# Graph network layer on one core: TensorE's first pass with a one-column second layer under a condition, and twelve empty instructions ahead of its loop

## Chip, cores and metric

One core of one Trainium2 chip. The time is the device time of one execution in microseconds. The kernel before took 271.45 us, the median of 3 runs (270.98 to 272.32).

## What is computed

There are 12,500 nodes with 128 features each, and 412,500 edges with 48 features each, sorted by the node they point at (`dst`). All nodes belong to one graph.

```python
h   = maximum(layernorm(x), 0)                       # 12500 x 128
agg = segment_sum(edge_attr, dst, 12500)             # 12500 x 48
u   = graph_globals[0]                               # 64
hid = relu(concat([h, agg, u]) @ W1 + b1)            # 12500 x 256
out = x + hid @ W2 + b2                              # 12500 x 128
```

Everything is f32.

## The kernel before

**Tiles.** The nodes are taken in 12 rounds of 1,024, and what is left is done in an epilogue. In each round the nodes are two blocks, A and B, of 512. The edges of a round are 11 groups of 3,072 rows in six slots (buffers e0 to e5, `SLOTS`), slot 4 with one group and the others with two.

**What a round does for the edges.** VectorE compares each edge's node with a row of numbers and so makes a one-hot matrix (`oh`, L666). TensorE multiplies edges and one-hots into windows of 28 nodes (`su`, L685, into PSUM banks `s`; even slots use one bank, odd slots the other). ScalarE copies the result to SBUF (`ss`, L689), and TensorE adds it at its place among the round's nodes (`pc`, L707, into banks `ax` and `ay`), with a second one-hot that VectorE makes (`pl`, L672). ScalarE copies the finished sums (`ag`, L750).

**What a round does for the nodes.** VectorE makes the statistics (`st`, L714, and small operations up to L731), ScalarE normalises (`xn`, L735), TensorE transposes (`tu`, L744), ScalarE copies (`hT`, L745). The first layer is `hh` (L754, from the nodes) and `ha` (L759, from the edge sums), in four PSUM banks `ph0`, `ph1`, `pt`, `po`, and a ReLU on ScalarE (`hi`, L764, into `hid`). The second layer `w2` (L780) multiplies `hid` by W2 into `ph0` for A and `ph1` for B, 8 matmuls of 128 columns each. VectorE adds the node's own row and b2, prepared by GpSimd as `xb` (L739), and keeps the result in `hold` (L784); all held rows are stored in the epilogue.

**The order.** A class `Flow` records every operation with what it reads and writes, and works out the semaphore waits. A round's body is written so that the second layer of round i stands in the body of round i + 1, behind the place matmuls of slots 5, 0 and 1. In round 0 there is no earlier round: the second layer there multiplies buffers that ScalarE has filled with zeros in the prologue, and VectorE writes the result into a held row that is written again later. TensorE's loop has its own shape: its body is cut at `su3`. It makes 13 passes, j = 0 to 12. The part from `su3` on stands first and is run if j > 0; then the prologue's part of TensorE, if j < 1; then the part up to the second layer, if j < 12. So in pass 0 TensorE runs the prologue, `su0` to `su2`, three placements and `w2A`, `w2B`, jumps back, and begins pass 1 with `su3`. In the order of the program, the jump stands right behind `w2B`, and the epilogue behind that.

**What waits for what around there.** `su5` writes the bank that the copy of `su3` reads. That copy stands in ScalarE's order behind the norms of A and B. The loads of the next x blocks are issued from ScalarE's queue, behind the copies `hT` and ahead of the copies `ag`; the load of a block waits until GpSimd's `xb` has read it, which starts when VectorE's `hold` has read the old `xb`. The edges come through SyncE's queue: each slot is loaded again when its `su` has read it.

In TensorE's order, matmuls stand as in the source; in the profile each f32 matmul is two weight loads and two matmul instructions (a transpose one of each).

Of the kernel before, what the change touches and what calls it, by code (L numbers as in the profile page):

```python
# [18 lines left out]
P = 128  # L19
# [9 lines left out]
R = 4  # L29
# [25 lines left out]
class Flow:  # L55
# [14 lines left out]
    def op(self, eng, name, reads, writes, emit, dma=False):  # L70
        self.seq.append(dict(eng=eng, name=name, r=tuple(reads), w=tuple(writes), emit=emit, dma=dma, it=self.at))
# [119 lines left out]
    def run(self):  # L191


        lo, hi = self.loop
        nc = self.nc
        start = [o for o in self.seq if o["it"] is None or o["it"] < lo]
        body = [o for o in self.seq if o["it"] == lo]
        end = [o for o in self.seq if o["it"] is not None and o["it"] > hi]
        for e in self.of:
            self.prepare(e)  # L200
        self.straight([o for o in start if o["eng"] != "PE"])
        regs = {}
        for o in body:
            for n, back in self.body.get(o["name"], []):
                u = self.unit(n)
                key = (o["eng"], u, (self.at_lo[n] - lo - back + self.extra[n]) * u)
                if key not in regs:
                    r = self.of[o["eng"]].alloc_register(f"w_{o['eng']}_{len(regs)}")
                    self.of[o["eng"]].reg_mov(r, key[2] + lo * u)
                    regs[key] = r  # L210

        def ahead(e):
            for n, c in sorted(self.ahead[e].items()):
                self.of[e].wait_ge(self.sem[n], (self.rank[n, c] + self.extra[n]) * self.unit(n))

        def repeat(o, i):
            waits = []
            for n, back in self.body.get(o["name"], []):
                u = self.unit(n)
                waits.append((self.sem[n], regs[(o["eng"], u, (self.at_lo[n] - lo - back + self.extra[n]) * u)]))  # L220
            self.emit(o, waits, i)

        def count(e):
            for (f, u, _), r in regs.items():
                if e == f:
                    self.of[e].reg_add(r, r, u)

        others = [e for e in self.of if e != "PE"]
        for e in others:
            ahead(e)  # L230
        every = {o["name"] for o in self.seq if o["it"] == hi}
        with nc.Fori(lo, hi + 1, 1, engines=[self.of[e].engine for e in others]) as i:
            for e in others:
                mine = [o for o in body if o["eng"] == e]
                for always, some in groupby(mine, lambda o: o["name"] in every):
                    with ExitStack() as last:
                        if not always:
                            last.enter_context(self.of[e].If(i < hi))
                        for o in some:
                            repeat(o, i)  # L240
            for e in others:
                count(e)
        own = [o for o in body if o["eng"] == "PE"]
        cut = [o["name"] for o in own].index(self.mark)
        with nc.Fori(0, hi - lo + 2, 1, engines=[nc.tensor.engine]) as j:
            with nc.tensor.If(j > 0):
                for o in own[cut:]:
                    repeat(o, None)
                count("PE")
            with nc.tensor.If(j < 1):  # L250
                self.straight([o for o in start if o["eng"] == "PE"])
                ahead("PE")
            with nc.tensor.If(j < hi - lo + 1):
                for o in own[:cut]:
                    repeat(o, None)
        self.straight(end)


# [149 lines left out]
def kernel(  # L408
# [12 lines left out]
    nc = tc.nc  # L421
# [4 lines left out]
    NH = H // P  # L426
# [19 lines left out]
    def bank(name):  # L446
        return psum.tile([P, BN], F32, name=name)
# [4 lines left out]
    ph = [bank("ph0"), bank("ph1")]  # L452
# [22 lines left out]
    hid = [const.tile([P, NH, r, P], F32, name=f"hid{k}") for k, r in two]  # L475
# [11 lines left out]
    w2 = const.tile([P, NH, D], F32)  # L487
# [25 lines left out]
    f = Flow(nc, tc)  # L513
    op = f.op
    A, B, Z = 0, 1, 2
# [62 lines left out]
    def dst_1(b):  # L578
        rows, n, g0 = dst_shape(b)
        d = di[b]  # L580
        k = f"di{b}"
        src = [k] + ([k + "r", k + "s"] if b == NB - 1 else [])
        op("DVE", f"fc{b}", src, [f"fc{b}"], lambda i: [nc.vector.tensor_copy(fc[b][:rows], d[:rows, 0:1])])
        k = b % DF
        op("DVE", f"df{b}", src + [f"fc{b}"], [f"df{k}"], lambda i: [
            nc.vector.tensor_scalar(df[k][:rows], d[:rows], fc[b][:rows], (V - 1) / 2, OP.subtract, OP.subtract)])
        op("DVE", f"mf{b}", [f"fc{b}", "m4"], [f"mf{b}"], lambda i: [nc.vector.tensor_scalar(mf[b][:rows], m4[:rows], fc[b][:rows], None, OP.mult)])

    def dst_2(b):
        rows, n, g0 = dst_shape(b)  # L590
        ob, ok = (ph[1], "PH1") if b else (S[0][:, P:], "S0")
        op("PE", f"of{b}", [f"mf{b}", "aq"], [ok], lambda i: [
            nc.tensor.matmul(ob[:, g0:g0 + n], aq[:rows].rearrange("c k n -> c (k n)"), mf[b][:rows, :n], start=True, stop=True, skip_group_check=True)])
        dv = df[b % DF].rearrange("c (p t) -> c t p", t=T)
        rv = rel[:, b * P * T:(b * P + rows) * T].rearrange("p (c t) -> p t c", t=T)
        for t0 in range(0, T, 3):
            key, bk = (("PT", pt), ("PH0", ph[0]), ("PO", po))[(2 * b + t0 // 3) % 3]
            pv = bk[:, :3 * P].rearrange("p (t c) -> p t c", t=3)
            op("PE", f"td{b}.{t0}", [f"df{b % DF}", "ident"], [key],
               lambda i, t0=t0, pv=pv: [nc.tensor.transpose(pv[:, t, :rows], dv[:rows, t0 + t, :], ident[:rows, :rows]) for t in range(3)])  # L600
            op("ACT", f"cd{b}.{t0}", [key], [f"rel{b}.{t0}"], lambda i, t0=t0, pv=pv: [nc.scalar.copy(rv[:, t0:t0 + 3], pv[:, :, :rows])])
# [190 lines left out]
    def prologue():  # L792
# [4 lines left out]
        for s in range(NS):  # L797
# [31 lines left out]
        blank = lambda name, key, dst_ap, shape: op("ACT", name, ["zero"], [key], lambda i: [  # L829
            nc.scalar.copy(dst_ap, zero[:shape[0]].to_broadcast(shape) if len(shape) == 2 else zero[:shape[0], :, None].to_broadcast(shape))])  # L830
        op("ACT", "c1", ["eps"], ["sc0"], lambda i: [nc.scalar.activation(sc[0][:, 0:1], eps, AF.Sqrt, bias=eps)])
        for k in (A, B):
            for a in range(NH):
                blank(f"hidz{k}.{a}", f"hid{k}.{a}", hid[k][:, a], [P, R, P])
            blank(f"xbz{k}", f"xb{k}", xb[k], [P, R, D])
        f.chain("DVE", "nm", [], ["nmod_i", "nmod"],
            lambda: nc.vector.tensor_scalar(nmod_i, nmod_i, NV - 1, None, OP.bitwise_and),
# [3 lines left out]
            lambda: nc.vector.tensor_reduce(a4, ident.rearrange("c (g k) -> c k g", k=CG), AX.X, OP.add),  # L841
            lambda: nc.vector.tensor_copy(aq, a4[:, :, None].to_broadcast([P, CG, NV])))
        op("DVE", "c3", ["iota_v"], ["iota_v"], lambda i: [nc.vector.tensor_scalar(iota_v, iota_v, 0.5, None, OP.mult)])
        for b in range(NB):
            dst_1(b)
            dst_2(b)
# [4 lines left out]
                             start=(t == 0), stop=(t == T - 1), skip_group_check=True)  # L851
# [120 lines left out]
    flags = nc.alloc_registers("bad")  # L972
    flag_of = {r.engine: r for r in flags}
    prologue()
    for it in range(NIT):
        body(it)
# [2 lines left out]
    ends = [f"ot{k}" for k in range(3)] + [f"x{k}" for k in (A, B)] + [f"hold{k}.{j}" for k in (A, B) for j in range(NIT - 1)]  # L979
    op("SP", "end", [], ends, lambda i: [nc.sync.nop(nofuse=True)])  # L980
    f.order((0, NIT - 1))
    f.mark = "su3"
    tc.mark_branch_hint_location("skip", engines=[ET.PE, ET.DVE])
    with tc.tile_critical(no_gpsimd_drain=True):
        f.run()
# [33 lines left out]
```

## Time and profile before

| what | value |
|---|---|
| median of 3 runs | 271.45 us (270.98 to 272.32) |
| profiled execution, its own time | 272.44 us |
| its span, first to last instruction | 270.7 us |
| busy: TensorE / VectorE / ScalarE / GpSimd | 92% / 88% / 47% / 20% |
| mean granted TensorE clock | 0.976 |
| DMA | 94.33 MB, mean 348 GB/s |

Rows of a timeline give the start in the span, the length, the engine, the line, the operation with output and input, and the number of instructions in a merged row; in brackets the idle time ahead of it and what ended that. Rows of the chain give start, length and what. Rows of stretches give, per engine in the order TensorE, its weight loads (PEld), VectorE, ScalarE, GpSimd, the busy time and the number of instructions, then the granted clock, the DMA share and GB/s. Rows of one line's instructions have shortest, median and longest duration in ns. Rows of the waits have the total in us, how often, and the longest. A row of a DMA queue has packets, MB and the share of time of 16 DMA engines.

### The profile page before, as it was taken

The numbers are of one execution on the slowest core, as the hardware profiler recorded it, in microseconds if no ns is written. First come the engines' busy times: TensorE is split into PE (matmuls) and PEld (weight loads), VectorE is DVE, ScalarE is ACT, GpSimd is POOL, SyncE is SP. The second block draws the span as 40 slices with busy tenths as digits, with TensorE's granted clock in tenths as the row PEclk, the third lists the DMA queues.
The fourth block names the chain that finished last, engine by engine and source line by source line (L and its number), as shares of the span: only waits on it lengthen the run. The fifth ranks groups of instructions, "written<-read, shape, count | busy, mean of one in ns | idle before, by whom it ended". The sixth has DMA issues, their size and how long they took to land.

```text
span 270.7 us, 17205 instructions
## 1 busy us (share of the span) xinstructions
PE 249.3 (92%) x7567; PEld 193.7 (72%) x7568; DVE 239.1 (88%) x591; ACT 127.6 (47%) x316; POOL 54.5 (20%) x47
## 2 busy tenths in 40 slices
PE   0853999999999999999999999999999999999990
PEld 0843894985977958949859769679589498597580
DVE  4699998998998999989989999989999899899511
ACT  6630524644545437337345445364383473454520
POOL 8100050050050230400500501403205005007000
PEclk9996699999999999999999999999999999999997
DMA  6999999999999999999999999999999999979911
GB/s 200 304 390 385 364 387 392 349 390 384 360 392 346 387 393 333 387 393 340 389 393 335 390 351 383 392 339 386 393 330 390 393 336 390 390 246 380 350 41 66
DMA packets 79012, 94.33 MB, mean 348 GB/s; under 512 B 3227, under 2 KB 72189, under 8 KB 78998
## 3 DMA queue, kind: packets, MB, share of 16 engines
q1 hardware_dynamic: 75398, 87.63, 92.4%
q10 hardware_dynamic: 3312, 6.03, 5.8%
q0 software_dynamic: 288, 0.49, 0.7%
q8 instruction: 7, 0.11, 0.2%
q14 instruction: 7, 0.06, 0.1%
HBM read 87.75 MB, written 6.40 MB: 348 GB/s over the span
## 4 chain that ended last, share of the span: by engine, by line
PE 88%; SPq 5%; DMA 3%; issue 1%; DVE 0%
PE s L685 27%; PE ph L780 18%; PE ph L754 8%; PE ax L707 8%; SPq L520 5%; PE ph L759 5%; PE pt L754 4%; PE po L754 4%; PE pt L759 4%; PE ay L707 3%; DMA e<-in_edge_attr_dram 3%; PE pt L744 3%; PE po L744 2%; PE s L942 1%; PE s L754 0%
## 5 line engine op out<-in xcount | busy, mean ns | idle before, releaser
L666 DVE TENSOR_TENSOR oh<-iota_v,rel_i 128x1344 f32<-128x1344 f32 (+1 forms) x78 | 130.5, 1712 | 0.3 <-PE s L685 0.3
L685 PEld LDWEIGHTS s<-e,oh 128*28 128x28 f32 x6336 | 73.2, 108 | 18.5 <-issue 16.4
L685 PE MATMUL s<-e,oh 128*28 128x48 f32 x6336 | 77.7, 208 | 7.5 <-issue 5.8
L739 POOL TENSOR_TENSOR xba<-xa,b_sb 128x512 f32<-128x512 f32 x12 | 15.5, 1290 | 193.6 <-DVE holda L784 193.6
L689 ACT COPY ss<-s 128x96 f32<-128x96 f32 (+1 forms) x72 | 17.0, 236 | 65.8 <-PE s L685 65.8
L672 DVE TENSOR_SCALAR pl<-iota_w,off_i 128x186 f32<-128x186 f32 x141 | 35.0, 308 | 0.5
L739 POOL TENSOR_TENSOR xbb<-xb,b_sb 128x512 f32<-128x512 f32 x12 | 31.1, 2594 | 0.0
L764 ACT ACTIVATE hida<-ph,bias 128x512 f32<-128x512 f32 x12 | 8.2, 687 | 41.4 <-PE ph L759 41.4
L780 PEld LDWEIGHTS ph<-w,hida 128*128 128x128 f32 x208 | 24.8, 195 | 3.9 <-issue 3.9
L707 PE MATMUL ax<-pl,ss 128*48 128x186 f32 (+3 forms) x172 | 27.3, 300 | 0.0
L780 PE MATMUL ph<-w,hida 128*128 128x128 f32 x208 | 27.3, 285 | 0.0
L707 PE MATMUL ay<-pl,ss 128*48 128x186 f32 (+3 forms) x168 | 26.4, 298 | 0.0
L780 PE MATMUL ph<-w,hidb 128*128 128x128 f32 x208 | 25.4, 275 | 0.0
L780 PEld LDWEIGHTS ph<-w,hidb 128*128 128x128 f32 x208 | 24.3, 192 | 0.0
L707 PEld LDWEIGHTS ax<-pl,ss 128*48 128x48 f32 x172 | 17.6, 126 | 4.3 <-issue 2.0
L735 ACT ACTIVATE xna<-xa,sha,sca 128x128 f32<-128x128 f32 x48 | 19.8, 484 | 1.0 <-DVE sha L731 1.0
L735 ACT ACTIVATE xnb<-xb,shb,scb 128x128 f32<-128x128 f32 x48 | 19.6, 481 | 0.0
L707 PEld LDWEIGHTS ay<-pl,ss 128*48 128x48 f32 x168 | 17.8, 124 | 0.0
L714 DVE BATCH_NORM_STATS2 sta<-xa 128x6 f32<-128x128 f32 x48 | 10.5, 280 | 6.1 <-DMA xa<-in_x_dram 6.1
L759 PE MATMUL ph<-ags,w1a 48*128 48x512 f32 x48 | 13.5, 641 | 0.0
L754 PE MATMUL ph<-hta,w1h 128*128 128x512 f32 x24 | 13.5, 645 | 0.0
L754 PE MATMUL po<-htb,w1h 128*128 128x512 f32 x24 | 12.3, 592 | 0.0
(150 smaller groups left out, 300.2 us busy)
## 6 DMA issues: line engine op xcount, KB each, us to landing
e<-in_edge_attr_dram SPq DMA_DIRECT2D x133, 576.0 KB, 7.7
xa<-in_x_dram ACTq DMA_DIRECT2D x11, 256.0 KB, 5.3
xb<-in_x_dram ACTq DMA_DIRECT2D x11, 256.0 KB, 5.8
out_dram<-holda SPq DMA_DIRECT2D x11, 256.0 KB, 3.5
out_dram<-holdb SPq DMA_DIRECT2D x11, 256.0 KB, 3.5
holda<-in_dst_dram SPq DMA_DIRECT2D x4, 384.0 KB, 5.0
e<-in_edge_attr_dram SPq DMA_DIRECT2D x1, 720.0 KB, 4.3
xa<-in_x_dram SPq DMA_DIRECT2D x1, 256.0 KB, 9.5
```

Of the source, the lines that this page charges most:

```text
L520: return [f.of[eng].dma_start(dst_ap(i) if callable(dst_ap) else dst_ap, src_ap(i) if callable(src_ap) else src_ap)]
L666: op("DVE", f"oh{name}", reads + ["iota_v"], [f"oh{name}"], lambda i: [nc.vector.tensor_tensor(ov, iota_v[:, None, None, :].to_broadcast([ ...
L672: nc.vector.tensor_scalar(out[:, j], iota_w, o[j], None, OP.is_equal) for j in range(len(o))])
L685: nc.tensor.matmul(S[k][NV * c:NV * c + V, j * DE:(j + 1) * DE], o[:, (j * CG + c) * T + t], ev[:, j * CG + c, t * DE:(t + 1) * DE], start ...
L689: op("ACT", f"ss{name}", [f"S{k}"], [f"ss{name}"], lambda i: [nc.scalar.copy(sv.rearrange("p j d -> p (j d)"), S[k][:, :m * DE])])
L707: out.append(nc.tensor.matmul(agg[bk][h:h + DE, at:at + w], sv[:, j], pv[:, j, frm:frm + w], start=bk in fresh and bk not in seen, stop=Tr ...
L735: nc.scalar.activation(xn[k][:m, r], xt[k][:m, r], AF.Relu, bias=sh[k][:m, r:r + 1], scale=sc[k][:m, r:r + 1]) for r in range(RR[k])])
L739: nc.gpsimd.tensor_tensor(xb[k][:m], xt[k][:m], b2_sb[:m, None, :].to_broadcast([m, RR[k], D]), OP.add)])
L744: op("PE", f"tu{k}", [f"xn{k}", "ident"], [key], lambda i: [nc.tensor.transpose(pv[:, r, :m], xn[k][:m, r], ident[:m, :m]) for r in range( ...
L754: nc.tensor.matmul(o, w1h[:, a * P:(a + 1) * P], hT[k][:, :, :m], start=first, stop=False, skip_group_check=True)])
L759: nc.tensor.matmul(o, w1a[h:h + DE, a * P:(a + 1) * P], ag[k // 2][h:h + DE, :, :m], start=False, stop=True, skip_group_check=True)])
L780: nc.tensor.matmul(ov[:m, r], hid[k][:, a, r, :m], w2[:, a], start=(a == 0), stop=(a == NH - 1)) for r in range(RR[k]) for a in range(NH)])
```

## The change

```diff
+        for _ in range(self.pad):
+            nc.tensor.nop(nofuse=True)
         own = [o for o in body if o["eng"] == "PE"]
...
             with nc.tensor.If(j < hi - lo + 1):
-                for o in own[:cut]:
-                    repeat(o, None)
+                for brief, some in groupby(own[:cut], lambda o: o["name"] in self.brief):
+                    some = list(some)
+                    if not brief:
+                        for o in some:
+                            repeat(o, None)
+                        continue
+                    with nc.tensor.If(j < 1):
+                        for o in some:
+                            repeat(dict(o, emit=self.brief[o["name"]]), None)
+                    with nc.tensor.If(j > 0):
+                        for o in some:
+                            repeat(o, None)
...
         for k in (A, B):
-            for a in range(NH):
-                blank(f"hidz{k}.{a}", f"hid{k}.{a}", hid[k][:, a], [P, R, P])
+            blank(f"hidz{k}", f"hid{k}.0", hid[k][:, 0, 0], [P, P])
...
+        op("DVE", "phz", [], ["PH0", "PH1"], lambda i: [nc.vector.memset(ph[k], 0.0) for k in (A, B)])
...
-    f.mark = "su3"
+    f.mark, f.pad = "su3", 12
+    f.brief = {f"w2{k}": lambda i, k=k: [nc.tensor.matmul(ph[k][:, 0:1], hid[k][:, 0, 0], w2[:, 0, 0:1], start=True, stop=True)] for k in (A, B)}
```

In pass 0 the second layer is one matmul of one column for each block, in place of 8 of 128 columns. In passes 1 to 11 it is as before, but behind a comparison of the pass number. VectorE clears the two banks in the prologue, and ScalarE clears only the part of `hid` that the short matmul reads. New lines move nearly all old ones behind them down by 12.

TensorE's order, from the last placements to the first instructions of the epilogue, before (`ax`, `ay`: sums in place; `ph_70`, `ph_71`: the banks ph0 and ph1; `w_143`: W2):

```order
L707 MATMUL ax<-pl_94,ss_100 48x186
L707 MATMUL ay<-pl_94,ss_100 48x186
L780 MATMUL ph_70<-w_143,hida 128x128 x8
L780 MATMUL ph_71<-w_143,hidb 128x128 x8
L253 UNCONDITIONAL_BRANCH
L245 REGISTER_ALU
L245 COMPARE_AND_BRANCH
L942 MATMUL s_65<-e_74,oh_87 28x48 x24
```

The same place in the changed kernel:

```order
L719 MATMUL ax<-pl_94,ss_100 48x186
L719 MATMUL ay<-pl_94,ss_100 48x186
L262 COMPARE_AND_BRANCH
L995 MATMUL ph_70<-w_143,hida 128x1
L995 MATMUL ph_71<-w_143,hidb 128x1
L262 UNCONDITIONAL_BRANCH
L265 COMPARE_AND_BRANCH
L792 MATMUL ph_70<-w_143,hida 128x128 x8
L792 MATMUL ph_71<-w_143,hidb 128x128 x8
L265 UNCONDITIONAL_BRANCH
L247 REGISTER_ALU
L247 COMPARE_AND_BRANCH
```

Two short matmuls, two comparisons and a jump are new ahead of the 16 matmuls of the second layer.

The start of TensorE's program up to the head of its loop, in the changed kernel:

```order
L1018 ISA
L1027 UNCONDITIONAL_BRANCH
L1027 BRANCH_PREFETCH_HINT
L1027 UNCONDITIONAL_BRANCH
L532 UNCONDITIONAL_BRANCH
L247 UNCONDITIONAL_BRANCH
L248 COMPARE_AND_BRANCH
L697 MATMUL s_66<-e_77,oh_90 28x48 x48
```

These are the rows of the kernel before with other line numbers: the twelve empty instructions of the source stand nowhere in TensorE's order.

VectorE's prologue in the changed kernel, from the last constants to the first use of `dst` (`holda` holds it there):

```order
L853 COPY aq<-a_157 128x128
L854 TENSOR_SCALAR iota_v<-iota_v 128x28
L855 MEMSET ph_70 128x512
L855 MEMSET ph_71 128x512
L595 CAST fc_159<-holda 128x1
L598 TENSOR_SCALAR holda<-holda,fc_159 128x768
```

The two memsets are new; the rows around them stand as before.

## Prediction

> **What bounds the kernel now.** I read the page's busy table and its chain that ended last, then the chain in order of time, then each engine's timeline around the first pass (15 to 46 us), where the change acts.
>
> ```profile
> PE 249.3 (92%) x7567; PEld 193.7 (72%) x7568; DVE 239.1 (88%) x591; ACT 127.6 (47%) x316; POOL 54.5 (20%) x47
> 24.19 0.85 PE s L685 x29
> 25.03 2.50 issue
> 27.53 1.64 PE s L685 x67
> 31.21 4.35 PE ph L780 x32
> 50.62 3.77 PE ph L780 x32
> 54.39 2.74 PE s L685 x240
> 64.52 0.42 PE pt L759
> 64.95 3.42 PE s L685 x284
> 69.46 3.77 PE ph L780 x32
> ```
>
> From 27.53 us on, the chain holds TensorE's work alone: each piece starts where the last one ended, and one pass takes 69.46 - 50.62 = 18.84 us. VectorE, with 88%, is close behind; what slack it has in a pass is worth as much as TensorE's own length. The row at 31.21 is the one the change removes: the second layer in pass 0, before any first layer has run, 32 matmul instructions for 16 matmuls (an f32 matmul is two).
>
> **The change part by part.** Pass 0 in TensorE's timeline, with three rows for the prices of what takes its place:
>
> ```profile
> 31.14 2.63 PE L780 MATMUL ph<-w,hida 128*128 128x128 f32 x16
> 35.49 2.81 PE L685 MATMUL s<-e,oh 128*28 128x48 f32 x240
> 38.22 0.65 PE L744 MATMUL pt<-ident,xna 128*128 128x128 f32 x4
> 44.13 1.13 PE L759 MATMUL ph<-ags,w1a 48*128 48x512 f32 x4
> 15.59 0.60 PE L860 MATMUL ph<-u,w1u 64*128 64x1 f32 x4
> 31.14 1.22 PE L780 MATMUL ph<-w,hida 128*128 128x128 f32 x4
> L780 PE MATMUL ph<-w,hida x208: 275/275/582, 31.1 to 261.4; 128*128 128x128 f32 x104
> 28.00:31.00 3.00, 3.00 (x67) 2.40 (x59) 2.84 (x10) 1.08 (x4) 0.00 (x0) 0.50 1.09 340
> 31.00:35.60 4.60, 4.60 (x44) 4.34 (x45) 4.53 (x10) 2.64 (x7) 0.00 (x0) 0.85 1.08 385
> ```
>
> *Removed and added.* The block runs from 31.14 to 35.49: 4.35 us. Two one-column matmuls, four instructions, replace it. The one-column row took 0.60 us for four; but the granted clock is 0.50 up to 31 and 0.85 on average over 31.00 to 35.60, so it is half until about 31 + 4.6 x 0.15 / 0.5 = 32.4. At that clock four instructions with the same weight load took 1.22 - 0.58 (the longest single one) = 0.64 from first start to fourth, 0.21 apart. So 0.60 to 0.85; I take 0.85, the row at the clock that holds there. The sums of slots 3 to 5 then start at 31.14 + 0.85 = 32.0: 3.5 us ahead.
>
> *Clock.* The first 0.4 us of these sums now run at half clock: 0.2 lost (0 if the clock returns early). The 240 instructions take 38.22 - 35.49 = 2.73: 1.09 for slot 3 (96 of them), 0.55 for slot 4, 1.09 for slot 5. Slot 5 could start at 32.0 + 0.2 + 1.64 = 33.8.
>
> *What is late next: ScalarE.* Slots 3 and 5 share a PSUM bank, so slot 5 waits for the copy of slot 3 (L689), which stands behind the norms on ScalarE.
>
> ```profile
> 32.01 1.63 ACT L735 ACTIVATE xnb<-xb,shb,scb 128x128 f32<-128x128 f32 x4
> 36.78 0.24 ACT L689 COPY ss<-s 128x96 f32<-128x96 f32 x1 [3.14 <-PE s L685]
> L520 SPq DMA_DIRECT2D e<-in_edge_attr_dram x1: 390/390/390, 24.7 to 24.7; - x1
> DMA to landing us min/median/max: 7.7/7.7/7.7
> ```
>
> The norms end at 33.64, set by VectorE and not by this change; the copy that now waits 3.14 us for TensorE would start there and end at 33.88. Slot 5 then starts near 33.95 instead of 33.8. Its last edges (issued 24.7, landed 7.7 later, 32.4) are there. The transposes start at 33.95 + 1.09 = 35.05: 38.22 - 35.05 = 3.15 us ahead.
>
> *Late after that: GpSimd.* The load of xb (in ScalarE's queue, ahead of the two copies L750 that L759 needs) waits until GpSimd has read the old xb.
>
> ```profile
> 35.24 0.68 DVE L784 TENSOR_TENSOR holda<-ph,xba 128x512 f32 x1
> 37.26 2.58 POOL L739 TENSOR_TENSOR xbb<-xb,b_sb 128x512 f32<-128x512 f32 x1
> 56.63 2.59 POOL L739 TENSOR_TENSOR xbb<-xb,b_sb 128x512 f32<-128x512 f32 x1
> 59.63 0.58 ACT L750 COPY ags<-ax 48x512 f32<-48x512 f32 x1 [0.80 <-POOL xbb L739]
> 60.23 0.58 ACT L750 COPY ags<-ay 48x512 f32<-48x512 f32 x1
> 62.97 1.13 PE L759 MATMUL ph<-ags,w1a 48*128 48x512 f32 x4
> ```
>
> GpSimd starts after VectorE's holda, which ran at 35.24 with no wait ahead of it, so it stays, and xbb ends at 39.84. In the next pass the copies began 59.63 - 59.22 = 0.41 after xbb and the second ended 1.59 after it; so in pass 0 it ends at 41.43. L759, now 44.13, could start at 44.13 - 3.15 = 40.98, but its second stream waits until about 41.45: 0.45 lost. What remains is 3.15 - 0.45 = **2.7 us**. In the second pass the same wait has 62.97 (the start of L759 there) - 60.81 = 2.2 of slack, less 2.7, plus what VectorE has gained by then (below): about even.
>
> *VectorE must follow.* It stands idle in each pass, 6.1 us in all, for xa, which is loaded behind TensorE's transposes:
>
> ```profile
> DVE sta L714 <- DMA xa<-in_x_dram: 6.1, 11, 1.0
> 46.49 0.87 DVE L714 BATCH_NORM_STATS2 stb<-xb 128x6 f32<-128x128 f32 x4
> 54.61 0.68 DVE L784 TENSOR_TENSOR holda<-ph,xba 128x512 f32 x1
> xb<-in_x_dram ACTq DMA_DIRECT2D x11, 256.0 KB, 5.8
> ```
>
> With xa issued earlier that 6.1 goes (1.0 in the first wait). What is left is a ring without TensorE: stb to the end of holda 55.29 - 46.49 = 8.8, then GpSimd 59.22 - 55.29 = 3.93, then xb's load 5.8: 18.5 us, just under 18.84. So VectorE follows, and the 2.7 lasts to the end, where ScalarE and VectorE wait for TensorE already.
>
> *The conditions.* Passes 1 to 11 now meet two compare-and-branches ahead of the real block. The trace has such rows at two places: where a pass begins (64.52 + 0.42 = 64.94, next piece 64.95: two compares and a jump) and at the loop's end (50.62 + 3.77 = 54.39, next 54.39). Nothing shows there: I read it as branches taken while matmuls already handed over still run. Ahead of the block those are the place matmuls, about 1.1 us of work; a wait of the weight loads stands there already:
>
> ```profile
> 50.55 1.86 PEld L780 LDWEIGHTS ph<-w,hida 128*128 128x128 f32 x16 [0.28 <-issue]
> ```
>
> So 0 to 0.28 a pass; I take 0, the rows with branches in them.
>
> *Prologue.* VectorE clears two banks, each at most the 0.68 of a 128x512 pass, in a gap:
>
> ```profile
> 2.77 0.17 DVE L843 TENSOR_SCALAR iota_v<-iota_v 128x28 f32<-128x28 f32 x1
> 4.17 0.15 DVE L583 CAST fc<-holda 128x1 f32<-128x1 int32 x1 [1.23 <-DMA holda<-in_dst_dram]
> ```
>
> At most 1.36 against the 1.23 of waiting, so 0 to 0.1 late, and later waits for dst follow; without that gap it would be 1.4 on VectorE. I take 0. ScalarE's clears only get shorter, ahead of the chain. The empty instructions leave no row in the built program (nothing stands for them in TensorE's order), so they cost nothing and shift nothing.
>
> Sum: 4.35 - 0.85 - 0.2 - 0.15 - 0.45 = 2.7. The profiled execution took 272.44 (span 270.7), 1.0 above the median of 271.45; taken off the median, **268.8 us**.
>
> **The rivals.**
>
> *The jump back is not covered.* TensorE's program arrives in blocks, seven packets in all:
>
> ```profile
> 21.15 1.76 PE L685 MATMUL s<-e,oh 128*28 128x48 f32 x97 [3.33 <-issue]
> q8 instruction: 7, 0.11, 0.2%
> q8 instruction: 1, 0.02, 68.1%
> q8 instruction: 1, 0.02, 68.8%
> ```
>
> The rows are the matmuls behind an earlier stop, all packets of the run, and those in the tenths of a microsecond from 25.1 and from 31.7. After the one at 25.1 TensorE, idle since 25.03, went on at 27.53, 2.4 later. The other lies in the middle of the block to be removed, whose 4.35 us would hide such a stop until 34.15. If the jump to the loop's head has to wait for it, the sums start at 34.15, 1.3 us ahead instead of 3.5, nothing else binds, and the time is 270.1. Against: TensorE ran 97 + 29 matmuls with their weight loads, 252 instructions, from one stop to the next; counted on by as much, the next block begins about 15 matmuls into the epilogue, and is what came at 31.7; the head of the loop has been there since the start, and no later pass fetches. The Trainium skill ("Runtime: NRT & Kernel Launch", section "Instruction fetch mechanics") says that a taken branch to a target outside a window of two pages stops until it is fetched; by that rule the stop is certain. The trace speaks against it: no packet came between 32 and 253 us, through eleven jumps back. Chance 0.14.
>
> *The branches show (slower).* If too little is handed over where the two compares stand, each of eleven passes pays for them. Up to 0.25 us a pass there is a gain left (11 x 0.25 = 2.7); from 0.37 (4.1 us) the kernel is over 0.5% slower; at 0.45, 4.95 - 2.7 gives 273.7. For it: no row shows a branch behind matmuls as short as the place ones. Against: the two boundaries with none. The Trainium skill ("Advanced Engine Details and Errata", section "Control Flow Timing") gives about 108 ns for a compare-and-branch; uncovered, an estimate of 11 x 2 x 0.108 = 2.4 us, and 271.1. Chance 0.14.
>
> *VectorE's ring binds.* Were xb's load 6.3 instead of 5.8, because edge loads released earlier queue ahead of it, the ring takes 19.0 a pass, over ten passes loses 1.6 or more, and little remains: 270.5 to 271.4. Against: those edge loads are then also further along when xb, issued at 39.84 as its buffer comes free, joins them. Chance 0.10.
>
> **How the numbers follow.** The main case has 0.60: its unknowns (0.25 less for the brief matmuls, 0.35 for clock and copy, 0.45 for GpSimd either way), not all at once, give 267.9 to 269.5. The other 0.02 is a mishap elsewhere. The range 267.9 to 271.0 takes in the uncovered jump and the mild half of the branches. A measurement of this kernel tells about 0.5%, 1.36 us, from no change. Faster by more: 0.58 of the main case, half of the jump (0.07), 0.04 of the branches: 0.69. Slower: 0.06 of the branches, 0.02 of the ring, 0.02 elsewhere: 0.10. The rest, 0.21, is the same.
>
> **What the changed profile would show.** Four L995 instructions near 31.1 and the sums of slots 3 to 5 from about 32.0; a short gap ahead of slot 5; the transposes near 35.05; sums of pass 1 at 43.35 instead of 46.05; 18.84 a pass after that; xa's waits gone on VectorE; the last matmul 2.7 us earlier. TensorE idle until 34 would be the jump; passes longer than 18.84 with idle ahead of the real block, the branches; L759 waiting in every pass, the ring. A gain over 3.2 would mean that GpSimd did not hold L759.

## The result, and the profile after

| | before | changed | ratio, 95% interval |
|---|---|---|---|
| median of the runs | 271.56 us (8 runs, 270.69 to 275.23) | 270.24 us (8 runs, 269.41 to 271.30) | 0.9948 (0.9929 to 0.9966) |
| the profiled execution | 272.44 (span 270.7) | 269.41 (span 267.6) | |

The kernel is a little faster: 1.3 us by the medians, where 2.7 was forecast, and 1.4 above the forecast of 268.8. The two profiled executions lie 3.0 us apart, because the one of before is among its longer ones and the one of the changed kernel is the shortest of eight.

The page of the changed kernel, the granted clock in its 40 slices and the shares of the chain that ended last:

```profile
PEclk9965799999999999999999999999999999999998
...
PE 87%; DVE 7%; issue 2%; ACT 1%; DMA 1%; DVEq 0%; SPq 0%
```

TensorE still sets the end, and its clock is below full in the third to fifth slice (13 to 33 us). TensorE's timeline from the stand-ins (L995, the two one-column matmuls that stand in for the second layer in pass 0) to the second layer of pass 2 (start, duration, line, shapes, idle before and its releaser):

```profile
30.19 0.38 PE L995 MATMUL ph<-w,hida 128*128 128x1 f32 x2
30.43 0.36 PE L995 MATMUL ph<-w,hidb 128*128 128x1 f32 x2
30.72 1.74 PE L697 MATMUL s<-e,oh 128*28 128x48 f32 x144
33.45 1.23 PE L697 MATMUL s<-e,oh 128*28 128x48 f32 x96 [0.98 <-ACT ss L701]
34.60 0.66 PE L756 MATMUL pt<-ident,xna 128*128 128x128 f32 x4
40.51 1.30 PE L771 MATMUL ph<-ags,w1a 48*128 48x512 f32 x3
43.03 3.49 PE L697 MATMUL s<-e,oh 128*28 128x48 f32 x288
47.54 2.05 PE L792 MATMUL ph<-w,hida 128*128 128x128 f32 x16
66.38 2.05 PE L792 MATMUL ph<-w,hida 128*128 128x128 f32 x16
```

The stand-ins take 30.72 - 30.19 = 0.53 us in place of 4.35. The sums go on at 30.72 with no stop at the jump back, slot 5 waits 0.98 for ScalarE's copy, and the sums of pass 1 begin at 43.03 instead of 46.05: 3.02 us earlier, of which about 0.4 is an earlier start of the first work on `dst` in this execution (TensorE's first matmul at 7.19, before at 7.58, with VectorE ahead of it). From there on a pass takes 66.38 - 47.54 = 18.84, as before.

The waits of the changed kernel (in all, times, longest), VectorE's clears in its prologue, and the first of ScalarE's two copies of the sums in pass 0:

```profile
ACT ags L762 <- POOL xbb L751: 13.4, 9, 3.5
DVE sta L726 <- DMA xa<-in_x_dram: 3.4, 7, 1.1
PEld ph L771 <- ACT ags L762: 1.1, 2, 0.8
```

```profile
3.04 1.03 DVE L855 MEMSET ph<- 128x512 f32 x2
4.15 0.15 DVE L595 CAST fc<-holda 128x1 f32<-128x1 int32 x1
```

```profile
39.88 0.58 ACT L762 COPY ags<-ax 48x512 f32<-48x512 f32 x1 [3.51 <-POOL xbb L751]
```

The clears fill the gap and the first use of `dst` comes at 4.15 (before 4.17). The copies wait 3.51 us for GpSimd, and TensorE's weight loads then wait up to 0.8 for the copies. So the waits are there as forecast, and this one execution gains about what the sum said (3.02 less 0.4, against 2.7); the question is where the median's other 1.4 us are.

### The profile page after: what moved, and what is told of

It is laid out like the page before. It is cut to its first block, busy times and chain, and to the rows that moved or that the text cites. A ratio compares the mean times of both kernels' runs of the same rounds, so it can differ in the third digit from the quotient of the medians.

```text
span 267.6 us, 17173 instructions
## 1 busy us (share of the span) xinstructions
PE 247.4 (92%) x7539; PEld 192.1 (72%) x7540; DVE 240.3 (90%) x593; ACT 126.5 (47%) x314; POOL 54.6 (20%) x47
## 4 chain that ended last, share of the span: by engine, by line
PE 87%; DVE 7%; issue 2%; ACT 1%; DMA 1%; DVEq 0%; SPq 0%
PE s L697 26%; PE ph L792 17%; PE ph L766 9%; PE ax L719 7%; PE ph L771 5%; PE po L766 4%; PE pt L766 4%; PE pt L771 4%; PE ay L719 3%; DVE oh L678 3%; PE pt L756 3%; PE po L756 2%; DMA holda<-in_dst_dram 1%; PE s L954 1%; DVE pl L684 1%
## 5 line engine op out<-in xcount | busy, mean ns | idle before, releaser
L697 PEld LDWEIGHTS s<-e,oh 128*28 128x28 f32 x6336 | 74.7, 109 | 17.7 <-issue 14.7
L697 PE MATMUL s<-e,oh 128*28 128x48 f32 x6336 | 79.3, 210 | 6.8 <-issue 4.3
L792 PEld LDWEIGHTS ph<-w,hida 128*128 128x128 f32 x192 | 22.3, 191 | 3.4 <-issue 3.4
L792 PE MATMUL ph<-w,hida 128*128 128x128 f32 x192 | 24.6, 281 | 0.0
L792 PE MATMUL ph<-w,hidb 128*128 128x128 f32 x192 | 23.4, 275 | 0.0
L792 PEld LDWEIGHTS ph<-w,hidb 128*128 128x128 f32 x192 | 22.4, 192 | 0.0
L771 PE MATMUL ph<-ags,w1a 48*128 48x512 f32 x48 | 14.1, 641 | 0.0
L762 ACT COPY ags<-ax 48x512 f32<-48x512 f32 x12 | 7.0, 580 | 15.0 <-POOL xbb L751 13.4
```

Of the source, the lines that this page charges most:

```text
L697: nc.tensor.matmul(S[k][NV * c:NV * c + V, j * DE:(j + 1) * DE], o[:, (j * CG + c) * T + t], ev[:, j * CG + c, t * DE:(t + 1) * DE], start ...
L771: nc.tensor.matmul(o, w1a[h:h + DE, a * P:(a + 1) * P], ag[k // 2][h:h + DE, :, :m], start=False, stop=True, skip_group_check=True)])
L792: nc.tensor.matmul(ov[:m, r], hid[k][:, a, r, :m], w2[:, a], start=(a == 0), stop=(a == NH - 1)) for r in range(RR[k]) for a in range(NH)])
```

## The experiments

Each batch of four ran on one chip beside runs of the kernel before. Three theories stood against each other: that the profile of before was an untypical one to subtract from; that the conditions cost something in each pass; and, from the second batch on, that TensorE's granted clock comes back at another time (theory 3). One number tells the profiles apart: the start of pass 1's sums. The table sets it against the span; the two last runs, narrow_x4 and wide_x4, come behind it:

| run | median us | ratio to before (95%) | profiled execution: clock full from | pass 1's sums start | span | span less start |
|---|---|---|---|---|---|---|
| before | 271.56 | 1 | 32.38 | 46.05 | 270.7 | 224.65 |
| before_again | 272.42 | 1.0012 (0.9991 to 1.0032) | 33.48 | 46.56 | 271.2 | 224.64 |
| cond_only | 272.14 | 1.0007 (0.9977 to 1.0037) | 31.28 | 45.54 | 271.6 | 226.06 |
| before_xb_late | 271.92 | 1.0014 (0.9978 to 1.0051) | 30.97 | 45.49 | 270.0 | 224.51 |
| changed | 270.24 | 0.9948 (0.9929 to 0.9966) | 29.69 | 43.03 | 267.6 | 224.57 |
| after_no_empty | 270.64 | 0.9934 (0.9908 to 0.9960) | 36.19 | 44.29 | 268.8 | 224.51 |
| after_again | 269.89 | 0.9930 (0.9904 to 0.9956) | 35.05 | 43.63 | 268.2 | 224.57 |
| wide | 269.65 | 0.9919 (0.9891 to 0.9946) | 30.31 | 43.23 | 267.8 | 224.57 |
| xb_late | 268.95 | 0.9892 (0.9866 to 0.9919) | 36.57 | 44.55 | 269.1 | 224.55 |
| xb_late_again | 269.02 | 0.9910 (0.9880 to 0.9940) | 30.65 | 42.74 | 267.2 | 224.46 |
| wide_xb_late | 268.91 | 0.9887 (0.9845 to 0.9929) | 31.55 | 42.60 | 267.2 | 224.60 |
| wide_xb_late_again | 269.57 | 0.9919 (0.9889 to 0.9949) | 31.70 | 43.31 | 267.8 | 224.49 |

Behind the start of pass 1's sums 224.5 to 224.65 us follow in every profile of the table but one (cond_only's, whose clock was below full again in its last three slices). So in these profiles the change and the edits act on pass 0 alone, and what differs between executions of one kernel does as well. How the time of the full clock is read comes below.

**before_again**: the kernel before, unchanged.

> The kernel before once more, so that a second profiled execution of it stands beside the first, which was 0.9 us above its median. Theory 1 (pinned start): after the change the transposes of pass 0 are tied to VectorE's norms, so an execution of the kernel before whose TensorE comes through its first pass sooner has less to gain; the missing 1.4 us of gain are then in pass 0 of ordinary executions: the sums of slots 3 to 5 start here 0.5 to 1.5 us before the 35.49 of the first profile, and 18.84 us a pass after that. Theory 2 (the conditions cost 0.12 us in each of eleven passes): pass 0 as in the first profile, 35.5 within 0.3. Ratio 1.000 by both.

272.42 us, ratio 1.0012 (0.9991 to 1.0032). Pass 0 in TensorE's timeline:

```profile
31.11 3.17 PE L780 MATMUL ph<-w,hida 128*128 128x128 f32 x16
35.99 2.81 PE L685 MATMUL s<-e,oh 128*28 128x48 f32 x240
```

The block took 35.99 - 31.11 = 4.88 us here, 0.53 more than in the first profile, since the clock came back at 33.48 instead of 32.38. The sums did not start earlier, as they should have if the first profile had been a late one. Over the four profiles that keep the full block (before, before_again, cond_only, before_xb_late) they start between 34.93 and 35.99, with the first one's 35.49 between them. So the first profile was not an untypical one, but the block's price is not one number.

**after_no_empty**: the changed kernel without the twelve empty instructions.

```diff
-    f.mark, f.pad = "su3", 12
+    f.mark, f.pad = "su3", 0
```

> The changed kernel without the twelve empty instructions. If they leave nothing in the program, it is the same program: ratio 0.995, within 0.002 of the changed kernel. If they do something (place the loop in the program), it differs by more than 0.3%. Its profile also gives a second execution of the changed kernel: by theory 1 the norms of pass 0 (end 33.28 in the first) and the transposes (34.60) come at the same distance from each other, and 18.84 us a pass; by theory 2 the passes are longer than 18.84 by 0.12.

270.64 us, ratio 0.9934 (0.9908 to 0.9960); its interval overlaps that of the changed kernel. The empty instructions do nothing that can be measured. But its profile shows another pass 0 than that of the same program above:

```profile
30.76 0.59 PE L995 MATMUL ph<-w,hida 128*128 128x1 f32 x2
31.21 0.57 PE L995 MATMUL ph<-w,hidb 128*128 128x1 f32 x2
31.70 4.83 PE L697 MATMUL s<-e,oh 128*28 128x48 f32 x240
```

The 240 matmul instructions of slots 3 to 5, 2.73 us in the profile of before, take 4.8: the granted clock is 0.50 until 36.19. From here the third theory came.

**cond_only**: the conditions with the real block under both, the long clear of `hid` kept, and no clear of the banks.

```diff
...
-    f.brief = {f"w2{k}": lambda i, k=k: [nc.tensor.matmul(ph[k][:, 0:1], ...)] for k in (A, B)}
+    f.brief = {o["name"]: o["emit"] for o in f.seq if o["name"] in ("w20", "w21") and o["it"] == 0}
```

> The conditions alone: the full second layer stands under both of them, nothing is saved and nothing is added in the prologue. Theory 1: the conditions cost nothing, ratio 1.000 within 0.002, passes of 18.84. Theory 2: eleven passes pay 0.12 each, ratio 1.005.

272.14 us, ratio 1.0007 (0.9977 to 1.0037), and 18.84 us a pass. The conditions cost nothing that can be measured. At the jump back of pass 0 its profile has a short stop that the profiles above don't have; narrow_x4 and wide_x4 come back to it:

```profile
34.99 2.80 PE L697 MATMUL s<-e,oh 128*28 128x48 f32 x240 [0.29 <-issue]
```

**xb_late**: the changed kernel, with the load of block B's x moved behind the two copies of the sums in ScalarE's queue, so that these no longer stand behind a transfer that waits for GpSimd.

```diff
             load_x(A, lambda i: (i + 1) % NIT * IN)
-            load_x(B, lambda i: (i + 1) % NIT * IN + BN)
...
         sums_out(B)
+        if it < NIT - 1:
+            load_x(B, lambda i: (i + 1) % NIT * IN + BN)
```

> The changed kernel with the load of xb behind ScalarE's two copies of the edge sums, so that these no longer wait for GpSimd. By the forecast's GpSimd term L771 of pass 0 starts 0.45 us sooner after the end of L766 and all later passes with it: ratio 0.993 (0.0017 below the changed kernel). If the term is wrong (the copies were not what L771 waited for), ratio as the changed kernel's, 0.995. If xb then comes too late for VectorE's statistics, 0.998 or more.

268.95 us, ratio 0.9892 (0.9866 to 0.9919), less than the changed kernel's so far. Its profile is again one with a late clock: the sums of slots 3 to 5 start at 31.86 and take 4.93, and the span is 269.1, while its other five runs are shorter. So the gain could be the moved load's or the clock's; the next runs ask for each by itself.

**wide**: the changed kernel with stand-ins of 128 columns.

```diff
-nc.tensor.matmul(ph[k][:, 0:1], hid[k][:, 0, 0], w2[:, 0, 0:1], start=True, stop=True)
+nc.tensor.matmul(ph[k][:, 0:P], hid[k][:, 0, 0], w2[:, 0], start=True, stop=True)
```

> One step of the change altered: the two stand-in matmuls of the first pass are 128 columns wide instead of one (all zeros times the weights, so the product is the same). Theory 3 (the clock): a stretch of about 3.4 us that holds the nearly idle one-column matmuls doesn't bring the full clock back, so in executions whose stretch ends between about 30.7 and 33 us the sums of slots 3 to 5 run at half clock to about 36 us (after_no_empty: 240 matmuls in 4.83 us instead of 2.8) and 1 to 2 us are lost. With 128 columns the clock should be back by 33.1 us at the latest, the sums of slots 3 to 5 should take under 4 us, and the time should be 0.4 to 1.0 below the changed kernel's: 269.2 to 269.9, ratio 0.990 to 0.993. Rival, the phase alone (when the stretches fall decides, whatever the matmuls hold): 270.2 to 270.7 again, ratio 0.994 to 0.996, and sums at half clock to 36 us in about half of the executions.

269.65 us, ratio 0.9919 (0.9891 to 0.9946): inside what theory 3 expected, and outside the 270.2 to 270.7 of the phase alone, though the interval overlaps those of the one-column kernels. TensorE's timeline of its profile:

```profile
30.62 0.49 PE L995 MATMUL ph<-w,hida 128*128 128x128 f32 x2
30.95 0.39 PE L995 MATMUL ph<-w,hidb 128*128 128x128 f32 x2
31.27 1.74 PE L697 MATMUL s<-e,oh 128*28 128x48 f32 x144
```

The wide stand-ins take 31.27 - 30.62 = 0.65 us, little more than the narrow ones (0.53 above). Ten of the eleven runs lie between 269.33 and 270.16. The profile itself says nothing on the columns: its clock was back at 30.31, ahead of the stand-ins.

**xb_late_again, wide_xb_late, wide_xb_late_again, before_xb_late**: xb_late again; both edits together, twice; and the move of block B's load in the kernel before.

> The kernel of xb_late again, on another chip if it comes so. If moving the load of block B gains by itself (the wait for GpSimd in the first pass, 0.45 by my sum, plus waits of VectorE for loads), ratio 0.988 to 0.991 again. If xb_late's runs only had the clock back early more often than those of the changed kernel (its six runs: one of 269.1 span at clock 0.955, five of 266.9 to 268.3 at 0.967 to 0.974), ratio 0.991 to 0.996.

> Both edits: 128 columns and block B's load behind the copies of the sums. Theory 3 and the GpSimd hold together: clock back by 33.1 us and no copy held by GpSimd: 268.4 to 269.2, ratio 0.986 to 0.990, the least of the four. If the clock's return doesn't hang on the columns: as xb_late, 0.989 to 0.992.

> The kernel before with block B's load moved alone. If the copies of the sums are held only where the pass before them is short (before: the copies waited 3.1 us for GpSimd in four places, 0.9 at most, and TensorE waited for none of it), it does nothing: 272.0, ratio 0.998 to 1.002. If the load's place in ScalarE's queue costs in every pass, it gains 0.5 or more: ratio under 0.998.

> The best version so far again: 128 columns and block B's load behind the copies of the sums. Theory 3: one group of runs, 268.5 to 269.2, ratio 0.986 to 0.990. Otherwise: some runs at 270.5 and above, as in xb_late and xb_late_again (one of six and four of twelve).

xb_late_again: 269.02 us, 0.9910 (0.9880 to 0.9940), eight runs at 268.55 to 269.22 and four at 270.45 to 270.74. wide_xb_late: 268.91, 0.9887 (0.9845 to 0.9929), all six at 268.48 to 269.15. Its repeat: 269.57, 0.9919 (0.9889 to 0.9949), five of six at 268.86 to 269.78 and one at 270.63; the expected single group at 268.5 to 269.2 was missed. Its profile is 0.57 behind that of xb_late_again at pass 1's sums (43.31 against 42.74) and shows a reason: slot 5 began at 34.33 instead of 33.76. The trace names ScalarE's copy for both waits, but in the repeat that copy had ended by 33.69, and the last edges of slot 5, issued at 26.82, landed 7.4 later, at 34.2. In the kernel before, the move does nothing that can be measured: 1.0014 (0.9978 to 1.0051), as expected of a kernel whose copies are held only 0.9 us at most.

Pass 0 with the load moved, from the profile of xb_late_again, shows what GpSimd's hold was worth, that is, the wait of ScalarE's copies for it:

```profile
33.76 1.23 PE L697 MATMUL s<-e,oh 128*28 128x48 f32 x96 [0.93 <-ACT ss L701]
40.82 1.13 PE L771 MATMUL ph<-ags,w1a 48*128 48x512 f32 x4
42.74 3.49 PE L697 MATMUL s<-e,oh 128*28 128x48 f32 x288
```

From the start of the first layer's part for the edge sums (L771) to pass 1's sums it is 42.74 - 40.82 = 1.92 us; in the changed kernel 43.03 - 40.51 = 2.52. The hold costs 0.60.

**after_again**: the changed kernel once more.

> The changed kernel itself, once more, beside the other three. All theories: 270.2, ratio 0.993 to 0.996. Theory 3 (the clock): its runs fall into two groups, 269.4 to 270.0 where the full clock is back before the one-column matmuls and 270.4 to 271.0 where it comes one stretch of 3.4 us later, with 3 to 6 in 10 in the second.

269.89 us, ratio 0.9930 (0.9904 to 0.9956). The two groups overlap more than expected: its profiled execution, 269.91, counts by its time to the first and had the clock back late. The pair that decides on the clock is this profile and that of wide_xb_late_again. First after_again, its timeline, and then three rows of stretches: two of 3.41 us and one of half a microsecond. Behind the start and end of a stretch stand its length and TensorE's busy time, and the column before the last two is the granted clock:

```profile
30.53 0.59 PE L995 MATMUL ph<-w,hida 128*128 128x1 f32 x2
30.98 0.56 PE L995 MATMUL ph<-w,hidb 128*128 128x1 f32 x2
31.48 4.40 PE L697 MATMUL s<-e,oh 128*28 128x48 f32 x240
43.63 3.49 PE L697 MATMUL s<-e,oh 128*28 128x48 f32 x288
```

```profile
28.22:31.64 3.42, 3.42 (x40) 2.67 (x33) 3.32 (x8) 1.71 (x6) 0.00 (x0) 0.50 1.09 351
31.64:35.05 3.41, 3.41 (x180) 3.41 (x179) 3.34 (x9) 2.35 (x7) 0.00 (x0) 0.50 1.08 389
35.00:35.50 0.50, 0.50 (x58) 0.50 (x53) 0.50 (x3) 0.00 (x0) 0.00 (x0) 0.95 1.09 392
```

Now wide_xb_late_again, the same two views, the stretch of 3.41 us and the half microsecond behind it:

```profile
30.49 0.80 PE L996 MATMUL ph<-w,hida 128*128 128x128 f32 x2
31.08 0.63 PE L996 MATMUL ph<-w,hidb 128*128 128x128 f32 x2
31.64 1.75 PE L697 MATMUL s<-e,oh 128*28 128x48 f32 x144
34.33 1.22 PE L697 MATMUL s<-e,oh 128*28 128x48 f32 x96 [0.94 <-ACT ss L701]
```

```profile
28.29:31.70 3.41, 3.41 (x29) 2.45 (x25) 3.31 (x8) 1.84 (x6) 0.00 (x0) 0.50 1.03 331
31.50:32.00 0.50, 0.50 (x33) 0.36 (x36) 0.50 (x2) 0.50 (x3) 0.00 (x0) 0.80 1.09 393
```

In these half-microsecond rows the clock is 0.50 or 1.00 except where it changes. So a row with 0.80 was at half for its first 0.20 us: the clock is full from 31.70 here, and from 35.05 in after_again (0.95 in the row from 35.00). It changes on a grid whose spacing the rows give: in the profile of before it fell at 22.14 and came back at 32.38, 10.24 apart, and in that of the changed kernel at 16.03 and 29.69, 13.66 apart, which is three and four times 3.41 (in narrow_x4, below, it came back at 30.46 and fell at 33.87, 3.41 apart):

```profile
22.00:22.50 0.50, 0.50 (x52) 0.50 (x42) 0.50 (x2) 0.00 (x0) 0.00 (x0) 0.64 1.09 394
32.00:32.50 0.50, 0.50 (x5) 0.50 (x5) 0.50 (x2) 0.50 (x3) 0.00 (x0) 0.62 1.01 364
```

```profile
16.00:16.50 0.50, 0.09 (x5) 0.12 (x9) 0.50 (x4) 0.00 (x0) 0.00 (x0) 0.53 1.08 389
29.50:30.00 0.50, 0.50 (x8) 0.41 (x4) 0.47 (x4) 0.00 (x0) 0.00 (x0) 0.81 1.09 334
```

The Trainium skill ("TensorE: Matmul & The Clock Gate", "Part 1: The HAM clock gate") has a window of 3413 ns that runs on freely, and a full clock after a busy one. The spacing of 3.41 us in these rows agrees with it. So after_again had a stretch from 28.23 to 31.64 and wide_xb_late_again one from 28.29 to 31.70, both with the same sums and placements in them, TensorE busy without a gap, and both stand-ins. The one with 128 columns brought the full clock, the one with one column did not, and the next stretch decided. Block B's load, the other difference between the two kernels, is issued only later in the pass.

The other profiles fit: where a stretch ended with at least 0.9 us of one-column matmuls in it (after_no_empty at 32.77, xb_late at 33.16, after_again at 31.64) the clock stayed at half for 3.41 more. Where it ended ahead of them or just in their beginning (the changed kernel at 29.69, wide at 30.31, xb_late_again at 30.65), or they were 128 wide (wide_xb_late at 31.55, and its repeat), it came back.

TensorE's busy time in these stretches says how much the one-column matmuls count for. First the changed kernel, then before_again:

```profile
26.28:29.69 3.41, 2.68 (x75) 2.50 (x77) 3.24 (x14) 0.83 (x3) 0.00 (x0) 0.50 1.09 354
```

```profile
26.65:30.07 3.42, 2.57 (x75) 2.39 (x77) 3.21 (x14) 0.79 (x3) 0.00 (x0) 0.50 1.07 349
```

With 2.68 us busy the full clock came back (at 29.69), with 2.57 it did not (at 30.07 it stayed at half). In all fourteen profiles (narrow_x4 and wide_x4 with them) every half-clock stretch that ended before 45 us with 2.68 or more brought it back, and none with 2.57 or less did, but for the three above: they were busy throughout and still did not. Without their 0.94 to 0.95 us of one-column matmuls they have under 2.5 us, so these counted as if TensorE had stood idle. That busy time alone doesn't decide shows in the prologue, too: in before_again the stretch from 13.00 to 16.41 was busy for 3.41 us, with transposes and small matmuls, and the clock fell at its end.

**narrow_x4 and wide_x4**: eight stand-ins instead of two, of one column and of 128.

```diff
-[nc.tensor.matmul(...)]
+[nc.tensor.matmul(...) for _ in range(4)]
```

> The stand-in of each block four times over (eight one-column matmuls in the first pass instead of two; the product is the same). It adds six matmuls of 0.2 to 0.3 us, 1.2 to 1.8 us. Theory 3: a stretch with 1.6 to 2.4 us of one-column matmuls counts as idle, so that the full clock comes back only after 34.5 us in nearly every execution, and sums of slots 3 to 5 run at half clock: 271.0 to 272.5, at least 0.7 above wide_x4, and the profile shows the 240 sums taking over 4 us or the clock at half past 34 us. Rival, phase alone: within 0.4 of wide_x4 or below it, since a one-column matmul is not longer than a 128-column one.

> The same eight matmuls, 128 columns wide. Theory 3: the clock is back by 33.1 us in every execution; six matmuls more cost 1.4 to 1.9 us on TensorE, of which up to 1.2 replaces the waits of the run called wide for ScalarE's copy (0.65) and GpSimd's addition (0.6): 269.9 to 271.0, runs in one group. Phase alone: as narrow_x4.

narrow_x4: 273.49 us, 1.0061 (1.0034 to 1.0089). wide_x4: 271.64, 0.9978 (0.9956 to 1.0001). The narrow ones are 1.85 us longer, as theory 3 had it and against the phase alone, but they lie 1.0 and 0.6 us above the ranges expected. The profiles show why; narrow_x4's execution was the longest of its runs, so only its pass 0 is read. First narrow_x4, its timeline and its clock, then wide_x4:

```profile
30.79 1.05 PE L995 MATMUL ph<-w,hida 128*128 128x1 f32 x8
31.70 1.03 PE L995 MATMUL ph<-w,hidb 128*128 128x1 f32 x8
34.88 5.02 PE L697 MATMUL s<-e,oh 128*28 128x48 f32 x240 [2.14 <-issue]
```

```profile
33.50:34.00 0.50, 0.00 (x0) 0.00 (x0) 0.50 (x3) 0.19 (x1) 0.00 (x0) 0.87 1.09 394
34.00:34.50 0.50, 0.00 (x0) 0.00 (x0) 0.43 (x3) 0.00 (x0) 0.00 (x0) 0.50 1.08 387
```

```profile
30.28 1.16 PE L995 MATMUL ph<-w,hida 128*128 128x128 f32 x8
31.28 1.06 PE L995 MATMUL ph<-w,hidb 128*128 128x128 f32 x8
34.04 2.80 PE L697 MATMUL s<-e,oh 128*28 128x48 f32 x240 [1.70 <-issue]
```

```profile
33.50:34.00 0.50, 0.00 (x0) 0.00 (x0) 0.50 (x3) 0.14 (x1) 0.00 (x0) 1.00 1.06 383
```

A stop stands ahead of the sums that none of these expectations had priced: 2.14 and 1.70 us in which TensorE waits for nothing but its own issue. That is the first rival of the prediction, the jump back that isn't covered, absent in the changed kernel and there with six matmuls more. In both the clock was full when the stand-ins began. With 128 columns it stayed full through the stop; with one column it fell at 33.87, and the 240 sums ran at half clock, 5.02 instead of 2.80 us. The stretch that ended there holds 1.14 us of the stop beside 1.9 us of one-column matmuls; the one of wide_x4, which ended near 33.1, 0.8 of the stop. So this pair shows the same as the other, with a small difference in the stop that I can't take out.

The stop goes with the fetching of the program. These two runs and cond_only, which has all 16 matmuls under both conditions, have one packet of instructions more than the seven of every other profile:

```profile
q8 instruction: 8, 0.13, 0.2%
```

It comes at 37.4 in cond_only, 37.3 in narrow_x4 and 36.5 in wide_x4; no other profile has one from 33 to 50 us. The packet ahead of it came at 31.5, 31.5 and 30.6, and TensorE went on with the sums at 34.99, 34.88 and 34.04, 3.3 to 3.5 us later in all three. The kernels with two stand-ins have a packet there too (31.2 in the changed one) and run on through it. So the jump was covered only while the program ahead of it was short enough: the prediction's margin of about 15 matmuls was too wide, as eight stand-ins in place of two already used it up. That the fetch causes the stop is likely by these times, but no run moved the packets alone.

## Why the prediction came out as it did

**The block removed.** 4.35 us in that profile, 4.88 in before_again and 34.93 - 31.16 = 3.77 in before_xb_late, whose timeline has these rows:

```profile
31.16 2.05 PE L780 MATMUL ph<-w,hida 128*128 128x128 f32 x16
34.93 2.81 PE L685 MATMUL s<-e,oh 128*28 128x48 f32 x240
```

It goes by when the clock returns (33.48 and 30.97): 4.35 was a middle value, and rightly the first term.

**The stand-ins.** 0.85 was forecast; 0.53 measured where the clock was already full, 0.94 and 0.95 at half clock (after_no_empty, after_again).

**The clock.** This is the step that failed: "The first 0.4 us of these sums now run at half clock: 0.2 lost (0 if the clock returns early)". It took the return at 32.4 from one execution as a fixed point, and saw no way for it to be later. But the grid lay elsewhere in every profile, and the edit itself put one-column matmuls there, which count as idle time in the stretch that holds them. Then the sums take 4.40 (after_again) or 4.83 us (after_no_empty) instead of 2.73: 1.7 to 2.1 lost, not 0.2. Some of it is had back, because sums that come later no longer wait for ScalarE and GpSimd: pass 1's sums start at 43.63 and 44.29 instead of 43.03, so 0.6 to 1.3 net. Two of the three profiles of the changed program are such executions. Where the clock returned alike early, the whole sum can be seen at once: from before_xb_late (30.97) to xb_late_again (30.65) pass 1's sums start 45.49 - 42.74 = 2.75 earlier and the span is 2.8 shorter. That is the edit's gain without the clock's late return and without GpSimd's hold; less 0.60 for the hold it is 2.15.

**The wait for ScalarE.** Forecast 0.15, measured 0.98: with the clock full from 29.69 the sums ran ahead, but ScalarE's norms still waited for VectorE and ended at 33.28 (before at 33.64), and the copy of slot 3 came behind them. It is the bound that the text had (slot 5 from 33.95; it began at 33.45, the transposes at 34.60 for 35.05), reached from an earlier start: it ate what the clock and the shorter stand-ins gave beyond the forecast, and cost nothing of the 2.7.

**GpSimd's hold.** Forecast 0.45, measured 0.60 (2.52 against 1.92), and nothing in executions with a late clock. Moving block B's load takes it away and does nothing to the kernel before; the medians of xb_late and its repeat are 268.95 and 269.02, so for the best version known the wait was worth taking away.

**The costs at nothing.** The conditions: cond_only, 1.0007 (0.9977 to 1.0037); the rival of slower branches falls. The Trainium skill ("Advanced Engine Details and Errata", "Control Flow Timing") gives about 108 ns for a compare-and-branch; cond_only shows none of it on the path. VectorE's clears: hidden, as argued. The empty instructions: nothing. VectorE's ring did not bind: a pass stayed at 18.84, and its waits for xa fell from 6.1 to 3.4, not to zero. The jump back: no stop in the changed kernel, whose sums follow the stand-ins at 30.72. By the rule of the Trainium skill ("Runtime: NRT & Kernel Launch", "Instruction fetch mechanics") a taken branch to a target outside a window of two pages stops until it is fetched. The changed kernel shows no such stop. cond_only and the runs with eight stand-ins show how near it was: they go on at 34.0 to 35.0, where the prediction put this rival's end at 34.15.

**The sum.** 2.7 was forecast for all executions. Early ones gain somewhat less: 3.02 at pass 1's sums, less the 0.4 of VectorE's and TensorE's earlier start, is 2.6 against the first profile, and the pair with the clock alike early gives 2.15, where the block removed was worth 3.77 and not 4.35. Late ones gain 0.6 to 1.3 less. The three medians of the changed program are 1.32, 1.40 and 2.14 us below those of before in their batches. Late returns in the share that the profiles suggest, about two in three, account for 0.4 to 0.9 of the missing 0.6 to 1.4; the block's lower price in early ones can account for some of the rest, which isn't told apart from the scatter of the medians. That the one-column matmuls cause the late return is shown by the pair of profiles and by the busy times of the stretches, and narrow_x4 against wide_x4 agrees; that wide (0.9919) is shorter than the changed kernel (0.9930 to 0.9948) in the median is likely, but the intervals overlap.

The measured 270.24 lies inside the range of 267.9 to 271.0 by luck. The main case ended at 269.5, and the part above it stood there for an uncovered jump and for mild branches, neither of which came; a late clock was not among the reasons for it.

The shortest of all was 128 columns with block B's load moved, 0.9887 (0.9845 to 0.9929) and 0.9919 (0.9889 to 0.9949), with xb_late, 0.9892 (0.9866 to 0.9919) and 0.9910 (0.9880 to 0.9940), not to be told from it.

## What to carry to other kernels

Where work on TensorE is removed while its clock is still at half, ask what the stretch looks like that has to bring the clock back, and fill a hole with matmuls that are as wide as the time allows: 128 columns cost 0.1 to 0.2 us more here than one (0.65 against 0.53, and 1.15 in wide_xb_late_again against 0.95 at half clock). A profile is one draw of the clock's grid; read where the clock changes in half-microsecond rows before a term is priced from it, and compare executions by a point behind the region, here the start of pass 1's sums. A gain on one engine is spent on the next waits in line (ScalarE's norms 0.98, GpSimd's hold 0.60), so price each of them from the earliest start that the gain can give.

## What the runs showed of the hardware

- A stretch of 3.41 us in which TensorE was busy without a gap, but for about 1 us with one-column matmuls, did not return the full clock (after_again, 28.23 to 31.64); with 128-column matmuls in their place it did (wide_xb_late_again, 28.29 to 31.70).
- At half clock, a stretch with TensorE busy for 2.68 of 3.41 us returned the full clock and one with 2.57 did not.
- A one-column f32 matmul with its own weights takes nearly as long as a 128-column one: 0.38 and 0.36 us against 0.49 and 0.39 for the two instructions each at full clock.
- Six matmuls more ahead of the jump back brought a stop of 1.7 to 2.1 us there. The three programs with a stop at that place (0.29 in cond_only) are the three with an eighth packet of instructions, at 36.5 to 37.4, and in all of them TensorE went on 3.3 to 3.5 us after the packet of 30.6 to 31.5.
